# Three layers of graph attention on one core: four instead of three tiles of each batch fetched by one-hot matmuls, and the query projection folded into one matrix

## The chip, the cores and the metric

The kernel runs on one core of one Trainium2 chip. The metric is the device time of one execution in microseconds (us); before the change it is 6761.06 us (median of three runs, 6731.34 to 6775.25). The profiled execution, from which all durations below come, took 6724.67 us.

## The reference

The inputs are 6250 nodes of 64 features, and 206250 edges, sorted by their destination, of 64 features each. Three layers of attention over edges follow each other, then a log-softmax, a residual and a layer norm:

```python
q = x @ Wq + bq;  k = x @ Wk + bk;  v = x @ Wv + bv;  e = edge_attr @ We
alpha = sum(q[dst] * (k[src] + e), -1) / sqrt(64)
w = softmax of alpha over the edges of one destination
x = relu(segment_sum((v[src] + e) * w, dst) + x @ Ws + bs)     # layer norm after layers 0 and 1
...
out = layernorm(x0 + log_softmax(x))
```

What costs is `x[src]`: every edge needs the row of its source node, in every layer, and the sources are random.

## The kernel before, in words

**Tiling.** Edges are cut into 403 chunks of 512 (four tiles of 128 edges), chunks into batches of four: a hundred full ones and one of three, per layer. A batch has a buffer `feat` with two halves, the source rows and the edge features. The raw features are gathered; weights are applied on the query side (`project`, L902, widens q by Wk and We with the matrix `eq`) and after the sums (`finish`, L954), so a chunk's work is a transpose, a score matmul, a softmax over a span of 32 destinations, and a weighted sum.

**Two ways to fetch source rows.** Of the 16 tiles of a batch most come by an indirect DMA each, issued by GpSimd (`gather`, L547, L553). A few are *picked* instead (`spots`, L543): TensorE multiplies the whole table of node rows, which stays in SBUF as two float32r halves (`parts`), by a one-hot matrix. With 49 blocks of 128 nodes, eight blocks to a PSUM bank, a pick is twelve matmuls of 512 columns (L863) and one of 128 (L854) into `ps_x`, of which there are two banks. VectorE then keeps the right one of eight blocks: a multiply (L873, into `rows_of_b`) and a reduce (L876, into `feat`). The one-hot matrices are made a batch ahead (`aim`, L824): a matmul of the key row (L830, into the only `ps_p` bank) and one compare of 128x896 per pick (L835, `hot`). `PICKS = 3`: the last tile of chunks 1, 2 and 3 of a batch is picked, so chunk 0 needs four gathers and the others three each. Layer 0 starts later (batch 4) and has one pick a batch up to batch 13 (`picked`, L513).

**Order of the work.** The five engines' streams are in the order in which the Python code issues them. A turn of the loop (L1274) handles batch u: weighted sums of batch u-2 on TensorE (L1155, copied out of the only `ps_g` bank by ScalarE, L1163), the transposed probabilities of u-1 (L1141, copied by VectorE, L1143), the scores of u (L1120, L1122; maximum L1129, exponential L1133), then four transposes of u's chunks (`turn`, L1105 in layer 0, L1110 later; ScalarE copies them, L1106 or L1113). Between the transposes stand the picks for batch u+1 (a generator, advanced by `some`, L1255, two half picks at a time), `aim` for u+2 and steps of side work (`project`, `finish`, `norm`).

**Gates.** After the copy of transpose j ScalarE copies four index columns into a small tile `gate` (L584, from `release`, called by `free`, L1269). The gathers of chunk j of batch u+2 read their indices from that tile, so they cannot start before it. GpSimd thus gets its work in four pieces a turn, each behind a ScalarE instruction that comes after a TensorE one.

**Side work.** For every group of four blocks `project` makes the queries: a transpose, `pq` (L911) and its copy with bias `qT` (L913), `pe` (L922) and its copy `qs` (L924), stored to `qq` in DRAM. `widen` (L689) makes `eq` from Wk and We.

Of the kernel before, what the change touches and what calls it, by code (L numbers as in the profile page):

```python
# [9 lines left out]
F32 = mybir.dt.float32  # L10
# [3 lines left out]
AF = mybir.ActivationFunctionType  # L14
ALU = mybir.AluOpType
# [3 lines left out]
P = 128  # L19
D = 64  # L20
L = 3
# [9 lines left out]
GS = 4  # L31
LB = 4
FB = 5
KB = 8
PICKS = 3
LEAD = (4, 1, 1)


# [376 lines left out]
def main_path(  # L415
# [53 lines left out]
    nc = tc.nc  # L469
# [6 lines left out]
    groups = [(g, min(GS, end - g)) for g in range(0, end, GS)] + [(end, NB - end)]  # L476
# [7 lines left out]
    batches = [(c, min(LB, NC - c)) for c in range(0, NC, LB)]  # L484
# [6 lines left out]
    const = ctx.enter_context(tc.tile_pool(name="const", bufs=1))  # L491
# [1 line left out]
    state = ctx.enter_context(tc.tile_pool(name="state", bufs=1))  # L493
    psum = ctx.enter_context(tc.tile_pool(name="psum", bufs=2, space=bass.MemoryType.PSUM))
    inputs = ctx.enter_context(tc.tile_pool(name="inputs", bufs=1))
    picks = ctx.enter_context(tc.tile_pool(name="picks", bufs=5))
    feats = ctx.enter_context(tc.tile_pool(name="feats", bufs=FB))
    tos = ctx.enter_context(tc.tile_pool(name="tos", bufs=3))
    turns = ctx.enter_context(tc.tile_pool(name="turns", bufs=1))
# [4 lines left out]
    nodes = ctx.enter_context(tc.tile_pool(name="nodes", bufs=2))  # L504

    def ps(tag):
        return psum.tile([P, 512], F32, tag=tag, name=f"ps_{tag}", bufs={"a": 3, "x": 2}.get(tag, 1))

    parts = inputs.tile([P, 2, NB, D], F32R, name="parts")
    start = turns.tile([P, NK * CH + NC], F32, name="start")  # L510
    MOST = PICKS

    def picked(layer, k):  # L513

        if batches[k][1] < LB or k < LEAD[layer]:
            return 0
        return 1 if layer == 0 and k <= len(groups) else PICKS

    eaT = dram.tile([D, NC * CH], F32, name="eaT")
    xts = [x] + [dram.tile([NB * P, D], F32, name=f"x{i}") for i in range(1, L)]  # L520
# [75 lines left out]
    for k in range(NK):  # L596
        n = min(P, NC - k * P)
# [4 lines left out]
    wq = const.tile([D, L, D], F32, name="wq")  # L602
    nc.scalar.dma_start(wq, Wq.rearrange("l i o -> i l o"))
    bqT = const.tile([D, L], F32, name="bqT")
# [29 lines left out]
    qq = dram.tile([P, (NB + 1) * P], F32, name="qq")  # L634
# [42 lines left out]
    for k in range(NK):  # L677
        n = min(P, NC - k * P)
# [6 lines left out]
        ends.rearrange("p c two -> p (c two)"), spans[:NC, :].rearrange("(o c) two -> o (c two)", o=1)  # L685
    )
    eq = const.tile([D, L, P], F32, name="eq")

    def widen(i):  # L689
        pw = ps("a")  # L690
        for h in range(2):
            nc.tensor.transpose(pw[:D, h * D : (h + 1) * D], ke[:, h, i, :], ident[:D, :D])
        nc.vector.tensor_copy(eq[:, i, :], pw[:D, :P])
        nc.tensor.transpose(pw[:D, P : P + D], wq[:, i, :], ident[:D, :D])
        wqT = turns.tile([D, D], F32, name="wqT")
        nc.vector.tensor_copy(wqT, pw[:D, P : P + D])
        nc.tensor.matmul(pw[:D, P + D : P + D + 1], wqT, bkT[:, i : i + 1], start=True, stop=True)
        nc.tensor.matmul(
            pw[:, P + D + 1 : P + D + 2],
            bqT[:, i : i + 1].to_broadcast([D, P]),  # L700
            bkT[:, i : i + 1],
            start=True,
            stop=True,
        )
        nc.vector.tensor_scalar(ws[:, i, D:], pw[:D, P + D : P + D + 1], D**-0.5, None, ALU.mult)
        nc.vector.tensor_scalar(sb[:, i, D:], pw[:, P + D + 1 : P + D + 2], D**-0.5, None, ALU.mult)
# [44 lines left out]
    assert NT <= P  # L751
    keyT = const.tile([P, MOST * P], F32R, name="keyT")
    one = const.tile([P, P], F32R, name="one")
    which = const.tile([P, MOST, NT, KB], BF16, name="which")

    def keys():

        nc.scalar.dma_start(src_b, src)
        yield
        key = turns.tile([P, CH], F32, name="place")[:, : MOST * NT].rearrange("p (s k) -> p s k", k=NT)  # L760
        spare = turns.tile([P, BITS + 1, CH], BF16, name="bits").rearrange("p b e -> p (b e)").bitcast(F32)
        spare = spare[:, : 3 * MOST * NT].rearrange("p (i s k) -> p i s k", i=3, k=NT)
        low, h = spare[:, 0], spare[:, 1:]
        tiles = src_b[:, : NT * LB * T].rearrange("p (k t) -> p t k", t=LB * T)
        nc.vector.tensor_copy(key, tiles[:, (LB - MOST + 1) * T - 1 :: T, :])
        nc.vector.memset(low, 0.0)
# [135 lines left out]
    def project(layer, g, n, y):  # L902

        pt = ps("a")
        for j in range(n):
            nc.tensor.transpose(pt[:D, j * P : (j + 1) * P], y[:, j, :], ident)
        xT = nodes.tile([D, GS * P], F32, name="xT")
        nc.vector.tensor_copy(xT[:, : n * P], pt[:D, : n * P])
        yield
        pq = ps("a")  # L910
        nc.tensor.matmul(pq[:D, : n * P], wq[:, layer, :], xT[:, : n * P], start=True, stop=True)  # L911
        qT = nodes.tile([D, GS * P], F32, name="qT")
        nc.scalar.activation(qT[:, : n * P], pq[:D, : n * P], AF.Identity, bias=bqT[:, layer : layer + 1])  # L913
        pk = ps("g")[:, : n * (D + 1)].rearrange("p (j c) -> p j c", j=n)
        for j in range(n):
            nc.tensor.matmul(pk[:, j, :], xT[:, j * P : (j + 1) * P], ws[:, layer, :], start=True, stop=True)
        nc.vector.tensor_tensor(
            sk[:, g : g + n, :], pk, sb[:, layer : layer + 1, :].to_broadcast([P, n, D + 1]), ALU.add
        )
        yield  # L920
        pe = ps("p")
        nc.tensor.matmul(pe[:, : n * P], eq[:, layer, :], qT[:, : n * P], start=True, stop=True)  # L922
        qs = nodes.tile([P, GS * P], F32, name="qs")
        nc.scalar.activation(qs[:, : n * P], pe[:, : n * P], AF.Copy, scale=D**-0.5)  # L924
        nc.sync.dma_start(qq[:, g * P : (g + n) * P], qs[:, : n * P])

    def begin(g, n):
        y = entered.get(g)
# [317 lines left out]
    def step(n=1):  # L1246
        for _ in range(n):
            advance()
# [3 lines left out]
        for _ in range(n):  # L1252
            advance(ending)

    def some(picking):  # L1255

        for _ in range(2):
            next(picking, None)

    ask(0, 0)  # L1260
# [4 lines left out]
    for layer in range(L):  # L1265
# [8 lines left out]
        for u in range(NU - 2):  # L1274
            close = u >= CLOSE
            this = chunks[layer, u]
            picking = pick(layer, u + 1)
            line.sums(u - 2)
            line.weights(u - 1)
            line.scores(u)  # L1280
            if waiting:
                active.append(waiting.pop(0))
            this.turn(0)
            free(u, 0)
            close_up(2) if close else close_up()
            ask(layer, u + 1)
            chunks[layer, u + 1].across()
            some(picking)
            aim(layer, u + 2)
            this.turn(1)  # L1290
            free(u, 1)
            line.store()
            close_up(2) if close else step()
            some(picking)
            if close:
                line.sums(u - 1)
                line.weights(u)
            this.turn(2)
            free(u, 2)
            line.store()  # L1300
            close_up(2) if close else step()
            some(picking)
            if close:
                line.sums(u)
            line.store()
            assert next(picking, None) is None
            this.turn(3)
            free(u, 3)
            close_up(2) if close else step()
# [101 lines left out]
```

## Time and profile before

| | us |
|---|---|
| median of three runs | 6761.06 |
| the profiled execution | 6724.67 |
| its span, first to last instruction | 6723.0 |
| TensorE matmul busy | 5225.9 (78%) |
| VectorE busy | 3220.8 (48%) |
| GpSimd busy | 3765.4 (56%) |
| ScalarE busy | 1479.2 (22%) |
| mean granted TensorE clock | 0.858 |

Busy time is a union of intervals; a matmul's duration includes its latency, so neighbours overlap. "Idle" is the time an engine stood still just before an instruction, and the name behind the arrow is what ended it. "remote" there means that the semaphore update which ended the wait is in the trace but could not be put down to an instruction that ended within it. The granted clock is the share of full speed that TensorE had in a stretch. GpSimd counts 0.94 us for a gather, but the next one starts 1.25 us after the last; the 0.30 us between are listed as "issue".

### The profile page before, as it was taken

To read this page: it belongs to the slowest core of one execution; us is meant where nothing else is said; L and a number is where in the kernel's file an instruction comes from. 1 tells how busy PE (TensorE), PEld (TensorE's weight loads), DVE (VectorE), ACT (ScalarE), POOL (GpSimd) and SP (SyncE) were. 2 spreads that over 40 slices of the span, in tenths; PEclk is the share of its full clock that TensorE was granted. 3 is DMA by queue.
4 is the path that set the end of the run, shared out by engine and by line. 5 is a ranking of instruction groups with operands and counts; after the bars stand their busy time and mean duration, and the time that the engine had idled before them with its cause. 6 is when DMAs were issued, how large, how long until landed. Compare 5 with 4: busy or idle time off the path is not lost.

```text
span 6723.0 us, 84981 instructions
## 1 busy us (share of the span) xinstructions
PE 5225.9 (78%) x24583; PEld 3475.7 (52%) x24583; DVE 3220.8 (48%) x5356; ACT 1479.2 (22%) x4460; POOL 3765.4 (56%) x3982
## 2 busy tenths in 40 slices
PE   5778888888888677877778877767777777777776
PEld 2455555555555345555555555534555555555553
DVE  3345454545555345554455555434445445445544
ACT  1112121211122222222222222221222222222222
POOL 6555555555655365555555655535555555555553
PEclk8688898888988788988888888878888888888887
DMA  6333333333333334444344444333344334333432
GB/s 141 91 78 84 84 84 84 84 82 82 87 85 81 75 75 81 85 85 84 81 82 83 85 84 84 82 70 71 79 82 81 80 79 82 79 80 78 81 79 61
DMA packets 1132761, 554.08 MB, mean 82 GB/s; under 512 B 946565, under 2 KB 1043963, under 8 KB 1113090
## 3 DMA queue, kind: packets, MB, share of 16 engines
q1 hardware_dynamic: 988834, 409.90, 27.5%
q0 software_dynamic: 127168, 130.47, 10.9%
q10 hardware_dynamic: 16288, 8.17, 0.6%
q8 instruction: 204, 3.34, 0.2%
q14 instruction: 267, 2.19, 0.1%
HBM read 451.48 MB, written 96.59 MB: 82 GB/s over the span
## 4 chain that ended last, share of the span: by engine, by line


## 5 line engine op out<-in xcount | busy, mean ns | idle before, releaser
L553 POOL DMA_INDIRECT feat<-x,gate x2598 | 2457.8, 946 | 1814.2 <-ACT gate L584 910.6
L863 PE MATMUL ps_x<-parts,hot 128*128 128x512 f32 x10344 | 3041.1, 442 | 503.0 <-issue 295.4
L863 PEld LDWEIGHTS ps_x<-parts,hot 128*128 128x128 f32 x10344 | 2130.3, 214 | 1091.1 <-issue 446.3
L553 POOL DMA_INDIRECT feat<-in_x,gate x1328 | 1261.3, 950 | 920.0 <-ACT gate L584 469.8
L873 DVE TENSOR_TENSOR rows_of_b<-ps_x,which 128x512 f32<-128x512 f32 x862 | 591.5, 686 | 1437.9 <-remote 652.2
L1113 ACT COPY featT<-ps_a 64x256 f32<-64x256 f32 x1612 | 589.4, 366 | 1735.0 <-remote 723.9
L876 DVE TENSOR_REDUCE feat<-rows_of_b 128x64 f32<-128x512 f32 x862 | 907.8, 1053 | 29.6
L1143 DVE COPY probT<-ps_p 128x512 f32<-128x512 f32 (+2 forms) x306 | 208.3, 681 | 1481.6 <-remote 1208.1
L835 DVE TENSOR_TENSOR hot<-ps_p,rank 128x896 fp32r<-128x896 f32 x862 | 883.5, 1077 | 7.7 <-PE ps_p L830 4.9
L1122 PE MATMUL ps_s<-featT,q 128*32 128x512 f32 x2418 | 560.5, 650 | 257.5 <-ACT featT L1113 112.3
L1155 PE MATMUL ps_g<-feat,probT 128*64 128x256 f32 x4848 | 662.6, 403 | 81.4 <-issue 57.2
L1155 PEld LDWEIGHTS ps_g<-feat,probT 128*64 128x64 f32 x4848 | 347.9, 142 | 318.2 <-issue 174.0
L1106 ACT COPY featT<-ps_a 128x512 f32<-128x512 f32 x403 | 234.7, 585 | 962.4 <-remote 400.5
L1163 ACT COPY part<-ps_g 128x256 f32<-128x256 f32 (+2 forms) x306 | 113.9, 372 | 1418.1 <-remote 1065.0
L1133 ACT ACTIVATE prob<-ps_s,part 128x512 f32<-128x512 f32 (+2 forms) x306 | 210.4, 688 | 756.0 <-DVE part L1131 323.5
L1110 PE MATMUL ps_a<-ident,feat 128*128 128x128 f32 x1612 | 349.6, 301 | 13.5 <-issue 8.9
L1122 PEld LDWEIGHTS ps_s<-featT,q 128*32 128x32 f32 x2418 | 80.1, 110 | 494.1 <-issue 267.5
L1129 DVE TENSOR_REDUCE most<-ps_s 128x1 f32<-128x512 f32 (+2 forms) x306 | 209.9, 686 | 239.1 <-remote 103.3
L1110 PEld LDWEIGHTS ps_a<-ident,feat 128*128 128x128 f32 x1612 | 192.7, 150 | 238.0 <-issue 181.1
L830 PE MATMUL ps_p<-keyT,one 128*128 128x384 f32 (+1 forms) x294 | 137.4, 467 | 201.7 <-DVE probT L1143 177.2
L1105 PE MATMUL ps_a<-ident,feat 128*128 128x128 f32 x1612 | 278.8, 299 | 15.1 <-issue 14.9
L1105 PEld LDWEIGHTS ps_a<-ident,feat 128*128 128x128 f32 x1612 | 197.1, 153 | 124.4 <-issue 103.5
(147 smaller groups left out, 2522.7 us busy)
## 6 DMA issues: line engine op xcount, KB each, us to landing
feat<-in_ea SPq DMA_DIRECT2D x300, 512.0 KB
featT<-eaT SPq DMA_DIRECT2D x200, 512.0 KB
eaT<-featT SPq DMA_DIRECT2D x100, 512.0 KB
feat<-x,gate POOLq DMA_INDIRECT x2598
feat<-in_x,gate POOLq DMA_INDIRECT x1328
part<-part SPq DMA_DIRECT2D x1209, 16.2 KB
q<-qq SPq DMA_DIRECT2D x1209, 16.0 KB
both<-part SPq DMA_DIRECT2D x66, 260.0 KB
```

The source lines that it names most:

```text
L553: nc.gpsimd.indirect_dma_start(out=feat[:, c, t, 0], out_offset=None, in_=xts[layer][:, :], in_offset=bass.IndirectOffsetOnAxis(ap=index[: ...
L835: nc.vector.tensor_tensor(hot, pk[:, s * P : (s + 1) * P].unsqueeze(1).to_broadcast([P, NH, P]), rank.unsqueeze(2).to_broadcast([P, NH, P] ...
L863: nc.tensor.matmul(px[:, : b1 - b0, :].rearrange("p b d -> p (b d)"), hot[:, h, :], parts[:, i, b0:b1, :].rearrange("p b d -> p (b d)"), s ...
L873: nc.vector.tensor_tensor(rows, px, which[:, MOST - n + s, k, :].unsqueeze(2).to_broadcast([P, KB, D]), ALU.mult)
L876: nc.vector.tensor_reduce(loaded[layer, k][:, LB - n + s, T - 1, 0], rows.rearrange("p b d -> p d b"), AX.X, ALU.add)
L1105: nc.tensor.transpose(pt[:, t * P : (t + 1) * P], self.feat(j)[:, t].rearrange("p h d -> p (h d)"), ident)
L1106: nc.scalar.copy(self.featT[:, j, :], pt)
L1110: nc.tensor.transpose(pt[:, t // 2 * P : (t // 2 + 1) * P], rows[:, t * D : (t + 2) * D], ident)
L1113: nc.scalar.copy(featT[:, :, h, :], pt[h * D : (h + 1) * D, : T // 2 * P].rearrange("d (i e) -> d i e", e=P))
L1122: nc.tensor.matmul(self.p_s[j * W : (j + 1) * W, :], self.q[:, j, :], self.featT[:, j, :], start=False, stop=True)
L1133: nc.scalar.activation(self.prob[:n], self.p_s[:n], AF.Exp, bias=neg, accum_out=self.part[:n, 0, P + 1 : P + 2])
L1155: nc.tensor.matmul(p_g[j * W : (j + w) * W, :w, :].rearrange("n c (h d) -> n c h d", h=2), self.probT[:, t, j * W : (j + w) * W], batch[:, ...
```

## The change

`PICKS` becomes a table by layer and batch, and says four in all of them; every batch that had three picks now has four, the last tile of every chunk, so that each chunk has three gathers. The batches with no pick or one keep that. `some` advances three half picks at a time instead of two. The pool of `hot` tiles grows from five to seven. To make room and save a step, `widen` multiplies the query matrix into `eq` and the query bias into a new column `be`, so that `project` needs one matmul and one copy for the queries in place of two of each. The matmuls for `sk` move behind the queries' store.

```diff
-PICKS = 3
+PICKS = ((4,), (4,), (4,))
...
-    picks = ctx.enter_context(tc.tile_pool(name="picks", bufs=5))
+    picks = ctx.enter_context(tc.tile_pool(name="picks", bufs=7))
...
-    MOST = PICKS
+    MOST = max(max(n) for n in PICKS)
...
-        return 1 if layer == 0 and k <= len(groups) else PICKS
+        return 1 if layer == 0 and k <= len(groups) else PICKS[layer][k % len(PICKS[layer])]
...
+    be = const.tile([P, L], F32, name="be")
...
-        nc.vector.tensor_copy(eq[:, i, :], pw[:D, :P])
+        room = picks.tile([P, KB, D], F32, name="rows_of_b", bufs=1).rearrange("p b d -> p (b d)")
+        e, wqT = room[:D, :P], room[:D, P : P + D]
+        nc.vector.tensor_copy(e, pw[:D, :P])
         nc.tensor.transpose(pw[:D, P : P + D], wq[:, i, :], ident[:D, :D])
-        wqT = turns.tile([D, D], F32, name="wqT")
         nc.vector.tensor_copy(wqT, pw[:D, P : P + D])
+        nc.tensor.matmul(pw[:D, 2 * P : 3 * P], wqT, e, start=True, stop=True)
+        nc.vector.tensor_scalar(eq[:, i, :], pw[:D, 2 * P : 3 * P], D**-0.5, None, ALU.mult)
+        nc.tensor.matmul(pw[:, 3 * P : 3 * P + 1], e, bqT[:, i : i + 1], start=True, stop=True)
+        nc.vector.tensor_scalar(be[:, i : i + 1], pw[:, 3 * P : 3 * P + 1], D**-0.5, None, ALU.mult)
...
-        pq = ps("a")
-        nc.tensor.matmul(pq[:D, : n * P], wq[:, layer, :], xT[:, : n * P], start=True, stop=True)
-        qT = nodes.tile([D, GS * P], F32, name="qT")
-        nc.scalar.activation(qT[:, : n * P], pq[:D, : n * P], AF.Identity, bias=bqT[:, layer : layer + 1])
+        pe = ps("p")
+        nc.tensor.matmul(pe[:, : n * P], eq[:, layer, :], xT[:, : n * P], start=True, stop=True)
+        qs = nodes.tile([P, GS * P], F32, name="qs", bufs=1)
+        nc.scalar.activation(qs[:, : n * P], pe[:, : n * P], AF.Identity, bias=be[:, layer : layer + 1])
+        nc.sync.dma_start(qq[:, g * P : (g + n) * P], qs[:, : n * P])
+        yield
         pk = ps("g")[:, : n * (D + 1)].rearrange("p (j c) -> p j c", j=n)
...
-        yield
-        pe = ps("p")
-        nc.tensor.matmul(pe[:, : n * P], eq[:, layer, :], qT[:, : n * P], start=True, stop=True)
-        qs = nodes.tile([P, GS * P], F32, name="qs")
-        nc.scalar.activation(qs[:, : n * P], pe[:, : n * P], AF.Copy, scale=D**-0.5)
-        nc.sync.dma_start(qq[:, g * P : (g + n) * P], qs[:, : n * P])
...
-    def some(picking):
-        for _ in range(2):
+    def some(picking, n):
+        for _ in range(-(-2 * n // 3)):
             next(picking, None)
```

The instructions of the loop stand in another order, too. TensorE, one turn in layer 1, from the first transpose of a batch to the last. Line 863 of before is 869 after the change, 854 is 860, 830 is 836 and 1110 is 1112. Before:

```order
L1110 MATMUL ps_a<-ident,feat 128x128 x2
L863 MATMUL ps_x<-parts,hot 128x512 x12
L854 MATMUL ps_x<-parts,hot 128x128
L830 MATMUL ps_p<-keyT,one 128x384
L1110 MATMUL ps_a<-ident,feat 128x128 x2
L863 MATMUL ps_x<-parts,hot 128x512 x12
L854 MATMUL ps_x<-parts,hot 128x128
L1110 MATMUL ps_a<-ident,feat 128x128 x2
L863 MATMUL ps_x<-parts,hot 128x512 x12
L854 MATMUL ps_x<-parts,hot 128x128
L1110 MATMUL ps_a<-ident,feat 128x128 x2
```

The same turn with the change:

```order
L869 MATMUL ps_x<-parts,hot 128x512 x12
L860 MATMUL ps_x<-parts,hot 128x128
L869 MATMUL ps_x<-parts,hot 128x512 x8
L836 MATMUL ps_p<-keyT,one 128x512
L1112 MATMUL ps_a<-ident,feat 128x128 x2
L869 MATMUL ps_x<-parts,hot 128x512 x4
L860 MATMUL ps_x<-parts,hot 128x128
L869 MATMUL ps_x<-parts,hot 128x512 x12
L860 MATMUL ps_x<-parts,hot 128x128
L1112 MATMUL ps_a<-ident,feat 128x128 x2
L869 MATMUL ps_x<-parts,hot 128x512 x12
L860 MATMUL ps_x<-parts,hot 128x128
```

Eight more matmuls stand before the key matmul, four and a closing one more between the second and the third transpose; between the third and the fourth nothing changes.

GpSimd's gathers of two batches in the same layer (the number behind `gate_` tells one gate from another). Before:

```order
L553 DMA feat_29152<-x1_105,gate_29179 128x64 x4
L553 DMA feat_29152<-x1_105,gate_29242 128x64 x3
L553 DMA feat_29152<-x1_105,gate_29273 128x64 x3
L553 DMA feat_29152<-x1_105,gate_29300 128x64 x3
L553 DMA feat_29315<-x1_105,gate_29342 128x64 x4
```

With the change:

```order
L553 DMA feat_31861<-x1_105,gate_31888 128x64 x3
L553 DMA feat_31861<-x1_105,gate_31961 128x64 x3
L553 DMA feat_31861<-x1_105,gate_32000 128x64 x3
L553 DMA feat_31861<-x1_105,gate_32027 128x64 x3
L553 DMA feat_32042<-x1_105,gate_32069 128x64 x3
```

One gather goes, the fourth behind a batch's first gate; the gates stay where they are. Over the program the gathers go from 3974 to 3690, the picks from 862 to 1146.

More of the change, by code (lines that the diff above doesn't have):

```diff
@@ L906, in project @@
             nc.tensor.transpose(pt[:D, j * P : (j + 1) * P], y[:, j, :], ident)
-        xT = nodes.tile([D, GS * P], F32, name="xT")
+        xT = nodes.tile([D, GS * P], F32, name="xT", bufs=1)
         nc.vector.tensor_copy(xT[:, : n * P], pt[:D, : n * P])
         yield
-        pq = ps("a")
-        nc.tensor.matmul(pq[:D, : n * P], wq[:, layer, :], xT[:, : n * P], start=True, stop=True)
-        qT = nodes.tile([D, GS * P], F32, name="qT")
-        nc.scalar.activation(qT[:, : n * P], pq[:D, : n * P], AF.Identity, bias=bqT[:, layer : layer + 1])
+        pe = ps("p")
[4 more added lines that the diff above has]
+        yield
         pk = ps("g")[:, : n * (D + 1)].rearrange("p (j c) -> p j c", j=n)
@@ L1277, in main_path @@
             picking = pick(layer, u + 1)
+            n = picked(layer, u + 1) if u + 1 < len(batches) else 0
             line.sums(u - 2)
@@ L1287, in main_path @@
             chunks[layer, u + 1].across()
-            some(picking)
+            some(picking, n)
             aim(layer, u + 2)
@@ L1293, in main_path @@
             close_up(2) if close else step()
-            some(picking)
+            some(picking, n)
             if close:
@@ L1301, in main_path @@
             close_up(2) if close else step()
-            some(picking)
+            some(picking, n)
             if close:
```

## The prediction

> **What bounds the kernel now.** I read the totals by engine first (table above): no engine is full, and TensorE's matmuls come closest. Then the groups of instructions, to see what each costs:
>
> ```profile
> L553 POOL DMA_INDIRECT feat<-x,gate x2598 | 2457.8, 946 | 1814.2 <-ACT gate L584 910.6
> L863 PE MATMUL ps_x<-parts,hot 128*128 128x512 f32 x10344 | 3041.1, 442 | 503.0 <-issue 295.4
> ```
>
> Then the waits, engine by engine:
>
> ```profile
> POOL feat L553 <- ACT gate L584: 1380.5, 339, 9.4
> DVE probT L1143 <- remote: 1208.1, 144, 18.6
> ACT part L1163 <- remote: 1065.0, 124, 14.0
> ```
>
> The gathers wait 1380.5 us for gates; VectorE and ScalarE wait over 1000 us each for something "remote". The timeline of one turn in layer 1 says what that is:
>
> ```profile
> 3499.68 0.39 PE L1155 MATMUL ps_g<-feat,probT 128*64 128x256 f32 x2
> 3499.99 0.66 PE L1141 MATMUL ps_p<-ident,prob 128*128 128x128 f32 x4
> 3506.28 0.37 ACT L1163 COPY part<-ps_g 128x256 f32<-128x256 f32 x1 [7.21 <-remote]
> 3509.19 0.94 POOL L553 DMA_INDIRECT feat<-x,gate  x1 [0.30 <-issue]
> 3511.93 0.69 DVE L1143 COPY probT<-ps_p 128x512 f32<-128x512 f32 x1 [9.45 <-remote]
> 3512.68 0.69 PE L830 MATMUL ps_p<-keyT,one 128*128 128x384 f32 x1 [5.53 <-DVE probT L1143]
> 3513.44 5.10 PE L863 MATMUL ps_x<-parts,hot 128*128 128x512 f32 x12
> 3515.08 0.19 ACT L584 COPY gate<-src_b 128x4 int32<-128x4 int32 x1
> 3515.54 0.94 POOL L553 DMA_INDIRECT feat<-x,gate  x1 [5.41 <-ACT gate L584]
> 3517.09 3.07 DVE L835 TENSOR_TENSOR hot<-ps_p,rank 128x896 fp32r<-128x896 f32 x3
> 3518.59 3.00 PE L863 MATMUL ps_x<-parts,hot 128*128 128x512 f32 x12
> 3521.80 1.95 PE L1155 MATMUL ps_g<-feat,probT 128*64 128x256 f32 x16
> 3530.51 0.94 POOL L553 DMA_INDIRECT feat<-x,gate  x1 [0.30 <-issue]
> 3533.96 0.37 ACT L1163 COPY part<-ps_g 128x256 f32<-128x256 f32 x1 [7.66 <-remote]
> 3534.02 0.69 DVE L1143 COPY probT<-ps_p 128x512 f32<-128x512 f32 x1 [8.23 <-remote]
> ```
>
> L1163 waits for L1155 alone, L1143 for L1141. The matmuls at 3500 end 6.2 and 11.3 us before their readers start, and L1155 of 3521.80 ends 10.2 us before its own. The readers start shortly after the run's last gather: L1143 2.74 us after 3509.19, both 3.5 us after 3530.51. TensorE's completions reach the other engines late while gathers run, and together when these stop; I take this as it stands, without its cause. ScalarE hangs in L1163 and issues no gate; GpSimd works off the gates it has (13 gathers, 3515.54 to 3531.45) and stops. Then completions arrive, L1143 frees `ps_p`, TensorE goes on, and the next gate is reached: 3.61 us from 3511.93 to 3515.54. A turn is thus the run of its gathers, 1.25 us each (0.94 and 0.30 of issue), plus some 5 us in which GpSimd stands still.
>
> Does that hold over the program? I cut out four stretches of whole turns; the first has about 15 gathers and one pick a turn, the others 13 gathers and three picks. First the engines' busy times and counts:
>
> ```profile
> core 0: us, PE busy (x) PEld busy (x) DVE busy (x) ACT busy (x) POOL busy (x), PEclk, DMA share, GB/s
> 121.50:368.00 246.50, 178.54 (x755) 101.92 (x755) 78.46 (x152) 48.12 (x131) 139.90 (x149) 0.70 0.40 94
> 379.00:2109.00 1730.00, 1432.61 (x7223) 996.68 (x7223) 881.43 (x1404) 344.92 (x970) 1005.97 (x1066) 0.89 0.37 82
> 2463.00:4286.00 1823.00, 1470.11 (x6951) 979.80 (x6949) 922.92 (x1464) 423.38 (x1364) 1063.45 (x1125) 0.88 0.41 83
> 4693.00:6558.00 1865.00, 1452.71 (x6716) 972.06 (x6709) 913.15 (x1494) 441.12 (x1377) 1053.26 (x1113) 0.86 0.39 80
> ```
>
> The same stretches for line 1129 alone, which comes once a turn (VectorE's busy time and count):
>
> ```profile
> 121.50:368.00 246.50, 6.86 (x10) 0.70 0.40 94
> 379.00:2109.00 1730.00, 56.30 (x82) 0.89 0.37 82
> 2463.00:4286.00 1823.00, 58.98 (x86) 0.88 0.41 83
> 4693.00:6558.00 1865.00, 58.88 (x86) 0.86 0.39 80
> ```
>
> A turn takes 24.65 us (246.5/10) with 14.9 gathers, then 21.10, 21.20 and 21.69 with 13.0, 13.1 and 12.9; the last three average 21.33 (5418/254). From the first stretch to the second 1.9 gathers went, two picks came, and a turn fell by 3.55 us (the first also carries the first `project`s, and a slower TensorE clock). So gathers set the turn up to here, and picks cost nothing that shows. TensorE idles 3.63, 4.10 and 4.79 us a turn in the three (1730.00 less 1432.61, over 82, and so on), on average 4.18; it is busy for 17.15.
>
> **The change part by part.** *Turns concerned:* batches 14 to 99 of layer 0 and 1 to 99 of the others, 86 + 99 + 99 = 284, one gather less and one pick more each.
>
> *Gather removed:* 1.25 us of a run of 13. If the 5 us around the run stay, 284 x 1.25 = 355 us off.
>
> *Pick added, TensorE:* per pick 12 x 294 ns (3041.1/10344, the union) and one L854 of 230 ns:
>
> ```profile
> L854 PE MATMUL ps_x<-parts,hot 128*128 128x128 f32 x862 | 198.6, 230 | 14.8 <-issue 14.3
> L876 DVE TENSOR_REDUCE feat<-rows_of_b 128x64 f32<-128x512 f32 x862 | 907.8, 1053 | 29.6
> L873 DVE TENSOR_TENSOR rows_of_b<-ps_x,which 128x512 f32<-128x512 f32 x862 | 591.5, 686 | 1437.9 <-remote 652.2
> L835 DVE TENSOR_TENSOR hot<-ps_p,rank 128x896 fp32r<-128x896 f32 x862 | 883.5, 1077 | 7.7 <-PE ps_p L830 4.9
> ```
>
> That is 3.76 us at the mix of clocks of before, and 3.2 at the full clock (3.00 for twelve at 3518.59, and the closing one). It goes into the idle 4.18 us, which the missing gather shortens to 2.93: 0.3 to 0.8 us a turn do not fit. Against that, busy time shrinks when the stops do. After the long stop at 3513.44 twelve matmuls take 5.10 us, at 3518.59 they take 3.00; and from the first stretch to the second busy time fell from 17.85 to 17.47 us a turn with two picks more, the clock going from 0.70 to 0.89.
>
> *Pick added, VectorE:* one `hot`, one multiply, one reduce, 2.8 us. VectorE's idle time covers them (10.7 of 21.33 us busy); without that cover they cost 284 x 2.8 = 795 us. What queues behind: four compares in a row (4.3 us) stand ahead of the second pick's multiply, which frees the `ps_x` bank that the fourth pick wants. In the turn shown they would fill 3517.09 to 3521.4, the multiply end at 3522.1, and TensorE, starting at half clock, want the bank at about 3519.5 (a third of a pick and a whole one after 3513.4): a stop of 2.6 us ahead of the fourth transpose. With TensorE at the full clock throughout and VectorE with nothing else ahead, it is about 0.6 (5.0 us of VectorE against 4.4 of TensorE). Both delay the fourth gate, while GpSimd comes to it 1.25 us sooner; but a stop of GpSimd lets completions through and shortens the next stop at the first gate. Together with what does not fit I let 0.7 us of the 1.25 be lost, 284 x 0.7 = 199 us. Bounds: nothing (first rival), or 1.87 us a turn (third rival).
>
> *Ends of layers:* after a layer's last gather two turns still pick with nothing to hide behind: 2 x 3.2 x 3 = 19 us added.
>
> *Queries:* 39 groups lose a matmul pair and a copy, 49.6/33 = 1.5 us of TensorE and 0.68 of ScalarE each:
>
> ```profile
> L911 PE MATMUL ps_a<-xT,wq 64*64 64x512 f32 x66 | 49.6, 832 | 49.2 <-issue 30.3 <-DVE xT L908 15.1 <-ACT gate L584 3.6
> L913 ACT ACTIVATE qT<-ps_a,bqT 64x512 f32<-64x512 f32 x33 | 22.5, 683 | 35.6 <-issue 19.8 <-PE ps_a L911 13.4 <-PE ps_a L1105 2.1
> 2276.38 0.37 SPq L1016 DMA_DIRECT2D x<-y  x1
> 2279.00 0.94 POOL L553 DMA_INDIRECT feat<-x,src_b  x1 [74.90 <-PE ps_a L911]
> ```
>
> Between layers they are off the path: the next layer's first gather follows the store of x at 2276.38, not the queries, whatever releaser the row names. In the loop the waits above cover them. Bounds: 0 and 39 x 2.2 = 86 us gained; I take 0. `widen` adds two small matmuls and two copies before the first scores, a loss of 0 to 3 us; I take 2.
>
> *Sum:* -355 + 199 + 19 + 2 = -135 us. From the profiled execution, 6724.67 (span 6723.0 and 1.67 around it), that gives 6590. That execution lies 36 us under the median shown, so the forecast for a median is 6761 - 135 = 6626, said as **6630 us**.
>
> **The rivals.** *The whole gather comes through.* Shorter runs hold completions back for less time, and TensorE stays at its full clock. For it: the fall of 3.55 us for 1.9 gathers. Against it: then picks rose into 6.8 us of idle a turn (246.50 less 178.54, over 10), now into 4.18. Time: 6761 - 355 + 21 = 6427. Chance 0.17.
>
> *Given back in full.* The late fourth gate costs all that the gather saves: 284 x 1.25 lost of 355 won, 6761 + 21 = 6782, which is no change (about 1% is what a measurement of this kernel can tell from none). For it: 355 us are only a quarter of today's waits for gates. Against it: the next first gate comes sooner after such a stop. Chance 0.22.
>
> *TensorE waits behind VectorE's compares: slower.* The stop ahead of the fourth transpose is between 0.6 and 2.6 us, 1.6 on average, and nothing else hides it: 17.15 + 3.2 + 1.6 = 21.95 us a turn, 0.62 over now and 1.87 over the first rival. 284 x 0.62 + 21 = 197, so 6958. It decides from a stop of 0.98 us on, where the sum passes 21.33. For it: only two `ps_x` banks, and completions already late. Against it: the half clock behind the 2.6 goes with the long stops. Chance 0.26.
>
> *VectorE blocks the gathers.* If GpSimd's issue stood still while VectorE reads two operands, 2.8 us more of VectorE would stretch the run: 284 x (2.8 - 1.25) + 21 = 461, so 7220. Against it: these two gathers start within the three compares of 3517.09 to 3520.16 and keep the step of 1.25.
>
> ```profile
> 3518.03 0.94 POOL L553 DMA_INDIRECT feat<-x,gate  x1 [0.30 <-issue]
> 3519.28 0.94 POOL L553 DMA_INDIRECT feat<-x,gate  x1 [0.30 <-issue]
> ```
>
> Chance 0.02. The Trainium skill (SBUF — State Buffer, "SBUF: two separate sides") has such a rule: some VectorE operations lock GpSimd out of a shared port, and it cannot write descriptors meanwhile. By that rule the time would be this rival's; the trace does not agree for these operations.
>
> **How the numbers follow.** Forecast 0.33, whole gain 0.17, given back 0.22, compares 0.26, block 0.02. Faster by over 1%: 0.33 + 0.17 = 0.5; within 1%: 0.22; slower: 0.26 + 0.02 = 0.28. The range runs from 6400, the whole gain and a third of the queries' bound, to 6930, just short of the slower case's middle. The forecast's own range, with 0.3 to 1.0 us a turn lost, is 6510 to 6710.
>
> **What would show it.** Gathers: 3690, still 1.25 us apart. Turns of about 20.8 us; TensorE busy for over 88% of them at a clock over 0.9; L1163 and L1143 still waiting for "remote". The stop at the first gate should shrink, those at the third and fourth grow. The compares' rival would show as TensorE waiting for the multiply ahead of the fourth pick, more than 1 us a turn. I am wrong if turns stay at 21.3 with TensorE idle as now, or if the gathers' step changes.

## The result and the profile after

| | before | after |
|---|---|---|
| median, us | 6755.73 (6731.34 to 6775.25, 4 runs) | 6508.92 (6465.84 to 6528.22, 4 runs) |
| ratio to before, 95% interval | | 0.963 (0.957 to 0.969) |
| profiled execution, us | 6724.67 | 6528.22 |
| mean granted TensorE clock | 0.858 | 0.936 |

247 us less, 3.7%, where 1% is about what can be told from no change. The forecast was 135 us less. The two profiled executions, from which the readings below come, differ by less, 196 us: the one before lies 31 us under its median, the one after 19 over.

First the groups of instructions of the changed kernel that answer to those shown of before (busy us, mean ns of one, idle time ahead and its releasers):

```profile
L869 PE MATMUL ps_x<-parts,hot 128*128 128x512 f32 x13752 | 3644.0, 416 | 497.3 <-DVE rows_of_b L879 285.1 <-DVE hot L841 110.9 <-issue 99.1
L553 POOL DMA_INDIRECT feat<-x,gate x2400 | 2276.7, 949 | 1825.7 <-ACT gate L584 990.3 <-issue 642.3 <-PE ps_s L1124 66.9
```

One matmul of a pick costs 265 ns in the union (3644.0/13752) instead of 294: the clock went up. GpSimd's idle time ahead of the gathers has not fallen, although there are fewer of them. Next, the waits (us in total, times, longest), again of the changed kernel:

```profile
POOL feat L553 <- ACT gate L584: 1510.2, 484, 12.4
ACT part L1165 <- remote: 379.2, 60, 25.4
DVE probT L1145 <- remote: 356.8, 65, 18.3
```

GpSimd stops ahead of a gate more often and for less time: 484 stops of 3.12 us on average, against 339 of 4.07. The two waits for "remote" that carried my argument fell to about a third, from 1065.0 and 1208.1 us. The stretches of whole turns (81, 86 and 86 of them, by the count of L1131) give the length of a turn; the first table has the busy time and count of each engine, the second L1131 alone:

```profile
core 0: us, PE busy (x) PEld busy (x) DVE busy (x) ACT busy (x) POOL busy (x), PEclk, DMA share, GB/s
442.80:2105.30 1662.50, 1534.12 (x8188) 1114.43 (x8188) 1096.60 (x1631) 342.05 (x950) 922.26 (x972) 0.97 0.35 84
2467.70:4241.20 1773.50, 1569.89 (x7981) 1117.14 (x7980) 1162.35 (x1716) 417.57 (x1350) 978.82 (x1032) 0.96 0.37 84
4599.60:6356.80 1757.20, 1560.86 (x7873) 1104.91 (x7873) 1162.65 (x1750) 440.90 (x1379) 979.55 (x1033) 0.96 0.38 84
sum 5193.20, PE 4664.87 PEld 3336.49 DVE 3421.60 ACT 1200.52 POOL 2880.63; mean PE 1554.96 PEld 1112.16 DVE 1140.53 ACT 400.17 POOL 960.21
```

```profile
442.80:2105.30 1662.50, 55.61 (x81) 0.97 0.35 84
2467.70:4241.20 1773.50, 59.18 (x86) 0.96 0.37 84
4599.60:6356.80 1757.20, 59.17 (x86) 0.96 0.38 84
```

A turn takes 20.53 us on average (5193.20/253; 20.52, 20.62 and 20.43 in the three), where it took 21.33. It still is a run of gathers, 12 x 1.25 = 15.0, plus a time in which GpSimd stands still: 5.53 us now, 5.08 before (21.33 less 13.0 x 1.25). TensorE is busy for 18.44 us of it (90%), with one pick more than in the 17.15 of before.

Sorted by gate over these stretches, from the rows of GpSimd's timeline, its stops are these (us a turn on average, beyond the 0.31 of issue):

| stop ahead of the | first gate | second | third | fourth | all |
|---|---|---|---|---|---|
| before | 3.44 | 0.66 | 0.46 | 0.49 | 5.05 |
| after | 2.50 | 1.00 | 0.67 | 1.28 | 5.45 |

The timeline at the end of a turn in layer 1 of the changed kernel still shows completions that come late:

```profile
3528.70 1.95 PE L1157 MATMUL ps_g<-feat,probT 128*64 128x256 f32 x16
3530.06 0.94 POOL L553 DMA_INDIRECT feat<-x,gate  x1 [0.30 <-issue]
3531.31 0.95 POOL L553 DMA_INDIRECT feat<-x,gate  x1 [0.30 <-issue]
3532.56 0.95 POOL L553 DMA_INDIRECT feat<-x,gate  x1 [0.30 <-issue]
3535.97 0.38 ACT L1165 COPY part<-ps_g 128x256 f32<-128x256 f32 x1 [6.32 <-remote]
3536.03 0.69 DVE L1145 COPY probT<-ps_p 128x512 f32<-128x512 f32 x1 [5.67 <-remote]
3538.97 0.19 ACT L584 COPY gate<-src_b 128x4 int32<-128x4 int32 x1
3539.43 0.95 POOL L553 DMA_INDIRECT feat<-x,gate  x1 [5.92 <-ACT gate L584]
```

The sums L1157 end at 3530.65, ScalarE reads them at 3535.97, 5.3 us later and 3.4 us after the last gather began.

### The profile page after: what moved, and what is told of

Same layout as the page of the kernel before. It is cut to its first block, busy times and chain, and to the rows that moved or that the text cites. A ratio compares the mean times of both kernels' runs of the same rounds, so it can differ in the third digit from the quotient of the medians.

```text
span 6526.5 us, 92238 instructions
## 1 busy us (share of the span) xinstructions
PE 5555.1 (85%) x28210; PEld 3923.4 (60%) x28210; DVE 4033.0 (62%) x6214; ACT 1465.0 (22%) x4421; POOL 3512.6 (54%) x3698
## 4 chain that ended last, share of the span: by engine, by line
## 5 line engine op out<-in xcount | busy, mean ns | idle before, releaser
L869 PE MATMUL ps_x<-parts,hot 128*128 128x512 f32 x13752 | 3644.0, 416 | 497.3 <-DVE rows_of_b L879 285.1
L869 PEld LDWEIGHTS ps_x<-parts,hot 128*128 128x128 f32 x13752 | 2594.9, 197 | 1139.0 <-DVE rows_of_b L879 332.7
L553 POOL DMA_INDIRECT feat<-x,gate x2400 | 2276.7, 949 | 1825.7 <-ACT gate L584 990.3
L553 POOL DMA_INDIRECT feat<-in_x,gate x1242 | 1189.3, 958 | 970.0 <-ACT gate L584 519.9
L879 DVE TENSOR_TENSOR rows_of_b<-ps_x,which 128x512 f32<-128x512 f32 x1146 | 788.4, 688 | 1050.1 <-PE ps_x L860 295.4
L841 DVE TENSOR_TENSOR hot<-ps_p,rank 128x896 fp32r<-128x896 f32 x1146 | 1169.1, 1081 | 170.3 <-PE ps_x L860 85.2
L882 DVE TENSOR_REDUCE feat<-rows_of_b 128x64 f32<-128x512 f32 x1146 | 1215.0, 1060 | 39.4
L1157 PE MATMUL ps_g<-feat,probT 128*64 128x256 f32 x4848 | 623.5, 398 | 110.1 <-DVE sk L925 74.8
L1157 PEld LDWEIGHTS ps_g<-feat,probT 128*64 128x64 f32 x4848 | 335.2, 141 | 312.5 <-issue 105.2
L1124 PE MATMUL ps_s<-featT,q 128*32 128x512 f32 x2418 | 458.8, 615 | 74.7 <-ACT featT L1115 45.0
L1131 DVE TENSOR_REDUCE most<-ps_s 128x1 f32<-128x512 f32 (+2 forms) x306 | 210.3, 687 | 276.8 <-PE ps_x L860 94.8
L1112 PE MATMUL ps_a<-ident,feat 128*128 128x128 f32 x1612 | 327.1, 285 | 6.8 <-issue 3.6
L1107 PE MATMUL ps_a<-ident,feat 128*128 128x128 f32 x1612 | 259.7, 286 | 0.0
L860 PE MATMUL ps_x<-parts,hot 128*128 128x128 f32 x1146 | 256.8, 224 | 1.8 <-issue 1.5
L860 PEld LDWEIGHTS ps_x<-parts,hot 128*128 128x128 f32 x1146 | 221.3, 193 | 53.3 <-issue 3.4
```

The lines of the kernel that those rows point to most:

```text
L553: nc.gpsimd.indirect_dma_start(out=feat[:, c, t, 0], out_offset=None, in_=xts[layer][:, :], in_offset=bass.IndirectOffsetOnAxis(ap=index[: ...
L841: nc.vector.tensor_tensor(hot, pk[:, s * P : (s + 1) * P].unsqueeze(1).to_broadcast([P, NH, P]), rank.unsqueeze(2).to_broadcast([P, NH, P] ...
L860: nc.tensor.matmul(px[:, : 2 * TAIL, :].rearrange("p (i b) d -> p i (b d)", i=2), hot[:, h, :], parts[:, :, b0:b1, :].rearrange("p i b d - ...
L869: nc.tensor.matmul(px[:, : b1 - b0, :].rearrange("p b d -> p (b d)"), hot[:, h, :], parts[:, i, b0:b1, :].rearrange("p b d -> p (b d)"), s ...
L879: nc.vector.tensor_tensor(rows, px, which[:, MOST - n + s, k, :].unsqueeze(2).to_broadcast([P, KB, D]), ALU.mult)
L882: nc.vector.tensor_reduce(loaded[layer, k][:, LB - n + s, T - 1, 0], rows.rearrange("p b d -> p d b"), AX.X, ALU.add)
```

## The experiments

The kernel before was timed beside every group of runs. Beside the first group (on chip 0) and the second (chip 1) it took 5167 and 5164 us, beside the others (chips 10 and 14) 6780 and 6732, which is nearer to its time in the result, whose chip is not on record. I call chips 10 and 14 and that of the result the late chips, 0 and 1 the prompt chips, after what their traces show below; where an expectation speaks of the first chip of the experiments, it means chip 0. Each group ran once, so whether the difference belongs to the chip or to something else about the run is not shown. Ratios are to the kernel before in the same group, so the prompt chips have a baseline of their own. No trace of the kernel before was taken there; the one with three picks stands in for it.

**One part alone, on a prompt chip.** The expectations of these four were written for a kernel of some 6760 us; beside them it took 5167, so only ratios and differences can be held against them.

The queries' part alone:

```diff
-PICKS = ((4,), (4,), (4,))
+PICKS = ((3,), (3,), (3,))
```

> The changed kernel with three picks as before (the queries by the joined matrix, the larger pool and the order of project stay). Theory, gathers set the turn: the queries lay beside other work, so 0 to 30 us off the kernel before, about 6740. Rival, the joined queries carry the gain: 100 us or more off, below 6660.

Measured: 5145.36 us, ratio 0.9963 (0.9949 to 0.9977).

The fourth pick on top of the gather that it replaces (the gather of chunk 0's last tile stays, and the pick goes to a scratch tile):

```diff
-            if (c, t) in spots(picked(layer, k)):
+            if (c, t) in spots(min(picked(layer, k), 3)):
...
+            to = loaded[layer, k][:, LB - n + s, T - 1, 0]
+            if n == 4 and s == 0:
+                to = picks.tile([P, D], F32, name="spill", bufs=1)
```

> The changed kernel with its four picks, but chunk 0's last tile is gathered as before and the fourth pick ends in a tile that nobody reads: 13 gathers and four picks a turn. It prices the pick alone. Theory: the pick costs what the change gave back of 355 us, 0.4 to 0.5 us a turn, 110 to 140 us over the queries-only kernel, about 6870. Rival, the busier TensorE at its full clock is the gain and the gathers do not matter: as fast as the change, about 6510.

Measured: 5559.41 us, ratio 1.0762 (1.0744 to 1.0780): 414 us over the run with the queries alone, 1.46 us a turn.

The gather left out, with no fourth pick for it:

```diff
+            if picked(layer, k) == 3 and (c, t) == (0, T - 1):
+                nc.gpsimd.memset(feat[:, c, t, 0], 0.0)
+                continue
```

> Three picks and 12 gathers a turn: the last tile of chunk 0 is neither gathered nor picked, a memset of GpSimd stands in the gather's place (those source rows are zeros). It prices the gather alone. Theory: 284 x 1.25 us less the memset's 0.1 to 0.2 us, 300 to 355 us off the queries-only kernel, about 6400. Rival, the clock of a busier TensorE is the gain: no change, about 6740.

Measured: 4815.89 us, ratio 0.9322 (0.9306 to 0.9337): 329.5 us under the run with the queries alone, 1.16 us a turn. The memset takes 0.17 us, but nearly all of it lies in the pause between two gathers: those around it start 1.28 us apart in place of 1.25. So 1.22 us a turn were on offer.

```profile
2512.00 0.94 POOL L556 DMA_INDIRECT feat<-x,gate  x1 [0.30 <-issue]
2512.94 0.17 POOL L554 MEMSET feat<- 128x64 f32 x1
2513.28 0.95 POOL L556 DMA_INDIRECT feat<-x,gate  x1 [0.16 <-issue]
```

The change with VectorE's compares spread, one behind each pick's reduce instead of four in a row, and `project`'s query matmul in another bank:

```diff
-            hot = picks.tile([P, NH, P], F32R, name="hot")
-            nc.vector.tensor_tensor(
...
+            compares.append((layer, k, s, pk))
...
+            compare()
             yield
...
-        pe = ps("p")
+        pe = ps("a")
```

> The change with the four compares that make the one-hot matrices no longer in a row: one after each pick's reduce, the rest at the end of the turn (project's query matmul takes another PSUM tag for it). If the multiply that stands behind four compares costs TensorE time (the changed profile has 285 us of matmuls waiting for that multiply and 111 for the compares), a third to all of the 285: 90 to 280 us off the change, 6230 to 6420. If the wait only takes the place of another one in the turn, within 40 us of the change, 6470 to 6550.

Measured: 6077.22 us, ratio 1.1765 (1.1745 to 1.1784), much slower. Its waits show why:

```profile
PEld ps_p L1151 <- DVE hot L848: 597.0, 276, 3.8
PE ps_p L1151 <- DVE hot L848: 472.4, 277, 3.6
```

L1151 are the transposes of the probabilities (L1143 in the change), which want the only `ps_p` bank; the compares now read it until the last pick's reduce is done, and TensorE stood behind them 277 times, 472.4 us in all. Compares in one row are cheaper than a bank held: this edit cures nothing and says nothing on the compares' queue by itself.

**The change itself, beside its neighbours.** The kernel of the result, unaltered:

> The changed kernel itself, unaltered, beside the kernel before on one chip. On the chip of the first four experiments the kernel before takes 5167 us instead of some 6760, and in their traces TensorE's completions reach the other engines at once. Theory A, the size of the gain hangs on late completions: where they come at once (before at 5167) the gain of 3.7% is gone. Adding up the parts measured there (5145 with the queries alone, 414 for a pick beside its gather, 330 off for a gather left out) gives 5229, ratio 1.012 to before. Rival B, a pick's 414 us are a bound by TensorE, which a gather less does not lift: 5450 to 5560, ratio 1.055 to 1.076. Rival C, the change gains 3.7% on any chip: ratio 0.96. If this run has the kernel before at some 6760, all three say 0.957 to 0.969, and the parts are to be measured again there.

> The change with three picks: only the queries by one matrix and the wider pool are left of it. On the first chip of the experiments it gave 0.996 to before. If this run has the kernel before at some 5167: the same, 0.995 to 0.998. If it has it at some 6760: my sum said the queries bring nothing there, 0.99 to 1.00; a rival is that they bring the upper bound of 86 us, 0.987 or less, and then a third of the whole gain is theirs.

Gates let go a batch earlier:

```diff
-            lead = 2 * LB if not layer else min(2 * LB, LB + u)
+            lead = 3 * LB if not layer else min(3 * LB, LB + u)
```

> The change, with every gate let go one batch earlier (three batches ahead of the transposes, not two). Where GpSimd stops ahead of gates (before at some 6760: 5.4 us a turn), theory A, the stops are what the late gates cost: they go, and the time falls by 5 us a turn towards 5100 to 5800, at most to TensorE's 18.4 us a turn. Rival B, the stops are what lets completions through: gathers run on without a stop, TensorE waits instead, and the time stays within 2% of the change or gets worse. Where completions come at once (before at some 5167), GpSimd with three gathers a chunk is no longer the bound, and A and B both say within 1% of the change.

Two picks instead of four:

```diff
-PICKS = ((4,), (4,), (4,))
+PICKS = ((2,), (2,), (2,))
```

> The change with two picks a batch instead of four: two more gathers, two picks fewer. If this run has the kernel before at some 5167, where GpSimd issues gathers nearly without a stop: one gather more than with three picks, 5145 + 330 = 5475, ratio 1.06, if gathers set the turn there; if TensorE's load sets it, it falls by 414 towards 4730, ratio 0.92. At some 6760: a gather more is 1.25 us a turn, 6755 + 355 = 7110, ratio 1.05, if the stops of 5 us stay; if a pick less gives TensorE's completions room, under 1.02.

These four met a prompt chip. Measured: the change 5545.46 us, ratio 1.0743 (1.0725 to 1.0761); the queries alone 5148.23, 0.9967 (0.9955 to 0.9980); earlier gates 5542.63, 1.0732 (1.0714 to 1.0750); two picks 5476.82, 1.0606 (1.0588 to 1.0624), which is the 5475 of gathers that set the turn. There the change is slower by 7.4%. My theory A, that the gain just goes, falls, and so does C, a gain on any chip. Rival B holds: with a gather less the change takes 5545 (1.0743), with that gather put back 5559 (1.0762), so its absence is worth some 10 to 14 us there, where with three picks a gather was worth 329.5.

The sums over the same 253 whole turns, in the order two picks, three (the queries alone), three with a gather left out, four with that gather, the change:

```profile
sum 4436.60, PE 3464.47 PEld 2239.28 DVE 2045.59 ACT 1210.76 POOL 3355.80; mean PE 1154.82 PEld 746.43 DVE 681.86 ACT 403.59 POOL 1118.60
```

```profile
sum 4129.50, PE 3769.92 PEld 2676.02 DVE 2745.73 ACT 1208.75 POOL 3126.05; mean PE 1256.64 PEld 892.01 DVE 915.24 ACT 402.92 POOL 1042.02
```

```profile
sum 3812.60, PE 3651.95 PEld 2632.31 DVE 2747.80 ACT 1202.99 POOL 2922.91; mean PE 1217.32 PEld 877.44 DVE 915.93 ACT 401.00 POOL 974.30
```

```profile
sum 4479.00, PE 4391.40 PEld 3211.38 DVE 3470.83 ACT 1204.51 POOL 3143.35; mean PE 1463.80 PEld 1070.46 DVE 1156.94 ACT 401.50 POOL 1047.78
```

```profile
sum 4475.50, PE 4388.48 PEld 3211.55 DVE 3473.30 ACT 1204.57 POOL 2894.11; mean PE 1462.83 PEld 1070.52 DVE 1157.77 ACT 401.52 POOL 964.70
```

Divided by 253, and set against 1.25 us for each gather that a full batch has:

| prompt chips | gathers' run | TensorE busy | turn |
|---|---|---|---|
| two picks, 14 gathers | 17.50 | 13.69 | 17.54 |
| three picks, 13 gathers | 16.25 | 14.90 | 16.32 |
| three picks, 12 gathers | 15.00 | 14.43 | 15.07 |
| four picks, 13 gathers | 16.25 | 17.36 | 17.70 |
| four picks, 12 gathers (the change) | 15.00 | 17.35 | 17.69 |

A turn is the larger of the two, within 0.4 us. With three picks GpSimd hardly stops (47.3 us ahead of gates in the whole program); the fourth makes TensorE the bound. Earlier gates change nothing: TensorE is busy for 98% of the change's turn there, and waits for gathers for 14 us in the whole program.

The waits and the timeline of the change on a prompt chip show what differs:

```profile
POOL feat L553 <- ACT gate L584: 890.2, 774, 11.7
ACT part L1165 <- PE ps_g L1157: 396.6, 303, 11.3
DVE probT L1145 <- PE ps_p L1143: 327.4, 291, 7.2
PE ps_x L869 <- DVE rows_of_b L879: 92.3, 191, 0.5
```

```profile
2816.30 0.95 POOL L553 DMA_INDIRECT feat<-x,gate  x1 [0.30 <-issue]
2816.39 1.95 PE L1157 MATMUL ps_g<-feat,probT 128*64 128x256 f32 x16
2817.61 0.94 POOL L553 DMA_INDIRECT feat<-x,gate  x1 [0.36 <-ACT gate L584]
2818.39 0.37 ACT L1165 COPY part<-ps_g 128x256 f32<-128x256 f32 x1 [1.04 <-PE ps_g L1157]
2818.86 0.94 POOL L553 DMA_INDIRECT feat<-x,gate  x1 [0.31 <-issue]
```

L1157 ends at 2818.34 and its reader starts 0.05 us later, in the middle of a run of gathers with a step of 1.25 to 1.31 us; no wait for "remote" is left. The Trainium skill (Perfetto Trace Analysis, "Summary: the profiler window per engine type") says that a TensorE row ends at an estimate, and that the time its semaphore then takes to reach the other engines does not show; a wrong estimate could look like a late completion. The pair of timelines speaks against that: the same instructions, by the same estimate, are read after 0.05 us here and after 5.3 us there.

**Late completions put in by hand.** ScalarE's and VectorE's copies read a column of the newest batch's last gathered tile first, so that they wait until the run has landed; once with three picks, once with four:

```diff
+            if c == LB - 1:
+                newest[layer] = k, loaded[layer, k][:, c, T - 2, 0, :1]
...
+            if newest.get(self.layer, (0,))[0] >= self.c // LB + 2:
+                seen = small.tile([P, 1], F32, name="seen_s")
+                nc.scalar.copy(seen, newest[self.layer][1])
             nc.scalar.copy(self.part[:n, :w, :P], p_g[:n, :w, :])
```

> The change with three picks, and late completions put in by hand: in each turn ScalarE's copy of the sums and VectorE's copy of the transposed probabilities first read one column of the newest batch's last gathered tile, so both wait until the run of gathers has landed, as they did on the chip of the result. Where the kernel before takes some 5167: theory A, a turn is the run of gathers plus a stop; the stop is the landing of 2.7 us and about 1.5 us of copies up to the next gate, less 1.25, so 3 us, and a turn of 16.3 becomes 19.3: 5148 + 284 x 3 = 6000, ratio 1.16 to before. Rival B, the copies have slack enough: ratio under 1.05. This run alone decides nothing on the change; it is the partner of the next.

> The same hold in the change with four picks. Theory A, it is the stop at the end of each run of gathers that lets a gather less pay: with the hold GpSimd's turn is 12 x 1.25 + 3 = 18 us, TensorE's 17.2 to 18.1 and partly behind the hold too; 18.3 to 19.0 a turn, 0.3 to 1.0 under the partner's 19.3, ratio of this to the partner 0.95 to 0.985, where without the hold it is 5545 / 5148 = 1.077. Rival B, four picks load TensorE so that it sets the turn with or without the hold, and the hold comes on top of it: ratio to the partner 1.03 or more. Between 0.985 and 1.03 the hold takes the loss away and gives no gain: A in half.

And the table at three, three, four:

```diff
-PICKS = ((4,), (4,), (4,))
+PICKS = ((3, 3, 4), (3, 3, 4), (3, 3, 4))
```

> The change with its table at three, three and four picks in turn, in every layer. Where the kernel before takes some 5167: with three picks GpSimd sets a turn (13 x 1.25 = 16.25 us, measured 16.3), with four TensorE (17.2 to 18.1). Theory A, buffers even out neighbouring turns: 12.67 gathers are 15.8 us, TensorE needs 14.9 + 2.4 / 3 = 15.7, so 16.0 a turn and 5060, ratio 0.98 to before. Rival B, each turn is bound by itself: (2 x 16.3 + 17.7) / 3 = 16.8 a turn, 5285, ratio 1.023. Where the kernel before takes some 6760: between the two kernels by its share of four picks, 0.985 to 0.99.

These met a late chip, where completions are late without the hold. Measured: 7240.93 us (ratio 1.0676, 1.0645 to 1.0708), 7113.41 (1.0488, 1.0455 to 1.0520) and 6697.38 (0.9880, 0.9849 to 0.9911). So the question for which the hold was made, whether it turns the sign on the prompt chips, was not put there, and stays open. What the pair says of a late chip: four picks stand to three as 0.982 (0.978 to 0.987, from the two intervals), a gain half as large as the change's 3.7% without the hold. The sums, three picks first:

```profile
sum 5866.20, PE 4467.53 PEld 3008.24 DVE 2723.18 ACT 1242.89 POOL 3111.84; mean PE 1489.18 PEld 1002.75 DVE 907.73 ACT 414.30 POOL 1037.28
```

```profile
sum 5742.70, PE 4892.03 PEld 3438.46 DVE 3420.09 ACT 1238.00 POOL 2864.18; mean PE 1630.68 PEld 1146.15 DVE 1140.03 ACT 412.67 POOL 954.73
```

A turn is 23.19 and 22.70 us; less the gathers' runs, GpSimd stands still for 6.9 and 7.7. So 0.8 us of the 1.25 are given back. That a longer stop puts more of TensorE's work behind it, of which four picks have more, is my reading; it was not tested. The mixed table falls where its share of fourth picks puts it, 1.2% under before.

**A gather less, beside four picks.**

```diff
+            if picked(layer, k) == 4 and (c, t) == (0, T - 2):
+                nc.gpsimd.memset(feat[:, c, t, 0], 0.0)
+                continue
```

> The change with four picks, and one more gather of chunk 0 left out in each of those 284 turns: a memset of 0.17 us on GpSimd stands in its place, so the source rows of that tile are zeros. It asks what a gather is worth beside four picks. Where the kernel before takes some 6760: theory A, a turn is the run of gathers plus stops, so 284 x (1.25 - 0.17) = 307 us come off the change's 6509: 6200, ratio 0.917 to before. Rival B, TensorE, busy for 18.4 of a turn's 20.5 us, already sets much of the turn: half of that or less, 6360 or more, ratio 0.94 or more. Where the kernel before takes some 5165: TensorE is busy for 17.2 to 18.1 of a turn's 17.6 to 18.1 us, so nothing comes off, 5530 to 5560, ratio 1.070 to 1.077; if gathers still set a part of the turn there, down to 5240, ratio 1.015.

Again a late chip: 6230.86 us, ratio 0.9256 (0.9229 to 0.9283), beside the change's 0.9628. The difference, 0.0372 of 6732, is 250 us, with some 43 either way from the two intervals. The expectation offered 307, with the memset at its full 0.17 us; here, too, the gathers around it start 1.28 us apart, so the offer was 284 x 1.22 = 346. Its sum over the 253 turns:

```profile
sum 4936.10, PE 4591.62 PEld 3303.35 DVE 3412.08 ACT 1201.01 POOL 2688.10; mean PE 1530.54 PEld 1101.12 DVE 1137.36 ACT 400.34 POOL 896.03
```

19.51 us a turn, 1.02 under the change, of 1.22 offered. So on the late chips the run of gathers still sets most of the turn beside four picks, with TensorE busy for 18.15 of the 19.51: between the two theories, and nearer A than B.

## Why the prediction was right, and where it was not

**What bounds the kernel: right for the late chips.** I read a turn as the run of gathers plus some 5 us in which GpSimd stands still. It was 5.08 before, 5.53 after and 5.7 with a gather less (19.51 less 13.75 and 0.03), and the gather left out gave 1.02 of 1.22 us.

**"If the 5 us around the run stay", 355 us off: too high by two or three tenths.** The gather's own term on the late chips, measured beside four picks, is 0.72 (250/346) to 0.84 (1.02/1.22) of its price, since the 5 us grew a little.

**The size.** With 247 us off, the result lies nearer to the first rival, the whole gain (334 off), than to the forecast (135 off). It is inside the range on record, and 1 us under the forecast's own range of 6510 to 6710.

**Pick added, "0.7 of the 1.25 be lost": mis-sized.** A turn fell by 0.80 us (21.33 to 20.53), so 0.45 was lost, 284 x 0.45 = 128 us instead of 199; by the medians, which lie 50 us further apart, it is less, down to 0.27. The failing step is "0.3 to 0.8 us a turn do not fit" into TensorE's idle time. I took a pick's 3.2 us against idle time that the missing gather shortens, and weighed the clock only loosely. TensorE's busy time rose by 1.29 us a turn with a pick more (17.15 to 18.44), since the clock, 0.86 to 0.89 before, was 0.96 and 0.97 after, and made the other three picks cheaper: 12 x 265 ns each, where it had been 12 x 294, which is 1.04 us a turn. The rest came from TensorE's other work; the scores alone fell from 560.5 us (L1122) to 458.8 (L1124). Everything fit: 2.09 us of a turn are left idle. The other part of the term, the stops, I had right in kind: by the table of gates the stop ahead of the first gate fell by 0.94 us, as I said, and those ahead of the second, third and fourth grew by 0.34, 0.21 and 0.79. Their sum, 0.40, is nearly the whole 0.45. So what was lost shows as stops ahead of the later gates, which come behind TensorE's picks and transposes, while TensorE's work as a whole did fit.

**L1163 and L1143 "still waiting for remote": only in part.** Both waits fell to a third. I had counted on shorter stops, not on fewer late completions. The run with a gather less beside four picks has them longer again, 531.3 us (ScalarE) and 622.1 (VectorE), with fewer stops ahead of gates (304 instead of 484). So a gather less does not seem to thin them out by itself; whether the fourth pick does, or the stops that it brings, was not tried.

**Queries at 0: right.** On the prompt chips they brought 0.35% (5145.36 and 5148.23), 22 and 16 us. On the late chips, if the picks' part goes by their number, the mixed table (-1.20%) and the change (-3.72%) leave (3 x -1.20 + 3.72)/2, about 0, with some 0.5% either way: inside the bounds of 0 to 86 us, and low in them.

**Ends of layers and `widen`, +21.** Outside the turns the profiled execution before spent 1305.0 us (6723.0 less 5418 in 254 turns), the one after 1333.3 with one turn more in it, so about 1313: +8. Some 31 of the 284 turns concerned lie in there, too; if they gained 0.80 us each, the ends by themselves cost about 33.

**The compares' rival.** It asked for a stop of more than 0.98 us a turn ahead of the fourth pick, on top of 17.15 + 3.2 of busy time. Before, the same wait was this:

```profile
PE ps_x L863 <- DVE rows_of_b L873: 200.0, 61, 14.3
```

After it is 285.1 (first fence), for all picks together: 0.70 us a turn became 1.00. Of its two terms the busy time failed, by 1.9 us, and the stop was smaller than 1.6. At the full clock, on a prompt chip, it never exceeded 0.5 us, where I had said 0.6.

**VectorE blocks the gathers: no.** With a pick's 2.8 us more of VectorE in a turn, gathers keep their 0.95 us and their 0.30 of issue. The rule that the prediction names beside this rival (the Trainium skill, SBUF — State Buffer, "SBUF: two separate sides") is for VectorE's two-port modes and for two inputs from SBUF. The compares and multiplies read one input from PSUM (`ps_p`, `ps_x`), so the second condition does not meet them, and no row shows whether they run in such a mode. Their keeping the step therefore does not speak against the rule.

**What I did not see.** The whole forecast rests on completions that reach the other engines late. That I took "as it stands, without its cause", and gave no chance to its being a state of some chips or runs. The sign came out right because the result was measured where completions come late; as I had not asked for that, it was luck to that extent. On the prompt chips the same change costs 7.4%: there GpSimd stands still for next to nothing with three picks, so a gather less helps only until TensorE's 17.35 us take over. That late completions are what separates the two signs is what both pairs of traces show side by side; it was not shown by turning it on or off.

## What to carry to other kernels

Ask of a turn which of two engines would set it if the other were free: work moved from one to the other pays only up to the point where their loads cross, here between three and four picks when completions are prompt. Where the profile shows idle time on both, that idle time hides the crossing, and the gain then belongs to the idle time as much as to the edit; time such a change under both conditions, if there are two, before keeping it. No version here was shown to be the best under both: four picks win on the late chips; on the prompt ones three picks with the joined query matrix do (0.997), a kernel that was not timed on the late ones.

## What the runs showed of the hardware

The same kernel took 6732 to 6780 us in some groups of runs and 5164 to 5167 in others (medians), with the same step of 1.25 us between gathers; in the traces of the former TensorE's completions are read up to several us late while gathers run (5.3 us in the turn shown), in those of the latter after 0.05 us. What makes them late stays open; no run with few or no gathers was made on the late chips.

The granted clock goes with how much of a turn TensorE is busy, on both kinds of chip. Layer 1's row on a prompt chip, with two picks, three, and the change (all engines' busy time; PEclk follows POOL's):

```profile
2022.80:3532.10 1509.30, 1160.83 (x5757) 742.88 (x5758) 693.36 (x1199) 418.58 (x1350) 1141.69 (x1207) 0.88 0.50 102
```

```profile
1919.50:3321.70 1402.20, 1270.73 (x6875) 894.60 (x6875) 930.54 (x1457) 418.71 (x1350) 1061.21 (x1119) 0.97 0.51 108
```

```profile
2081.00:3598.60 1517.60, 1475.90 (x7993) 1072.35 (x7994) 1178.44 (x1715) 417.84 (x1350) 979.96 (x1040) 1.00 0.48 98
```

77% busy goes with 0.88, 91% with 0.97, 97% with 1.00; on the late chips 81% with 0.88 (before) and 89% with 0.96 (after). The Trainium skill (TensorE: Matmul & The Clock Gate, "Part 1") says that a monitor sets the clock gate by how busy TensorE has been lately; the rows agree. So a pick seems to pay part of its own price by keeping the clock up, which my sum for it weighed too lightly; no run changed the clock by itself.
